# Where the first loads of a two-layer LoRA kernel are held: the second half of block 0 and the experts' weights

## The chip, the cores and the metric

The kernel runs on one NeuronCore of one Trainium2 chip. The metric is the device time of one execution in microseconds (us), lower is better. Of the kernel before there are three timed runs, and one further execution was recorded by the hardware profiler.

## The reference

`x` holds 64 sequences of 64 tokens with 1024 features, in float32. Layer 0 adds to every sequence the output of its own rank-16 adapter; layer 1 adds a dense layer and a mixture of eight rank-16 experts, of which the two with the largest logits are used for each token.

```python
# layer 0: A, B chosen for each sequence by itok_B_4_50
Bx = einsum('bni,bri->bnr', x, B[ids0]);  x = x + einsum('bnr,bor->bno', Bx, A[ids0])
# layer 1: language_ids = itok_B_0_7
base   = einsum('btd,od->bto', x, W)
logits = einsum('btd,ed->bte', x, Wr) + 5.0 * one_hot(language_ids)
gates  = two largest logits of each token, softmax over the two
h      = einsum('btd,erd->bter', x, A)
x = x + base + 2.0 * einsum('bter,bte,eor->bto', h, gates, B)
```

## The kernel before

The 4096 tokens are cut into eight blocks of 512. Tokens are columns: a block of `x` is 1024 features by 512 tokens, held as two tiles `("x", k, 0)` and `("x", k, 1)` of four feature groups each (1 MB a tile). Two feature groups are a quarter of a block, 512 KB. The blocks are worked in four pairs. For each pair the dense layer is a fast matrix product with seven block products instead of eight (the tiles `ti`, `t`, `s`, `sf`, `pa`, `pb`, `pf` belong to it); for the first pair one product is done whole (`pw`).

For each block, in the order of the data:

- `gather` on POOL brings 128 rows of `B` (`gb`) and of `A` (`ga`), 512 KB each, by indirect DMA.
- `turn`: TensorE transposes `gb` (`pt`), ScalarE copies it out (`bt`).
- `project`: TensorE multiplies `bt` with the first and then the second half of the block (`pb`), VectorE masks the result (`bx`).
- `adapt`: TensorE multiplies `ga` with `bx` (`px`), VectorE adds it into `x`.
- `rows`: TensorE multiplies the adapted `x` with the experts' weights `a1_sb` (`ph`), ScalarE copies `h`; then `gates` on VectorE, and `weigh` transposes on TensorE (`pg`).

The order in which each engine issues its work is not written by hand. Every step is given to `Plan.add` with its engine and cost, the keys that it reads and writes, a due number `at` (lower is more urgent), buffers that it takes, and, for a DMA, its size. `Plan.order` (lines 64 to 167) plays these through once: at each turn it takes the engine that can start first and, among its steps that can start within `LOOK` = 0.2 of that, the one with the lowest `at`. A DMA's end is set by one running total (`moved`, 350 KB a unit of time) plus `LAND` = 1.8. The result is a fixed program order on each engine; what the chip then does with it, it does in its own time, and an instruction whose input is late holds up all behind it on its engine.

At the start the order of the loads is steered with small copies on POOL that wait for one DMA and write one column into the target of the next, so that the next DMA's issue on SP must wait for the copy:

- `hold` in `load` (line 368) keeps the whole second half of block 0 until the first quarter of block 0 has landed.
- `hold` in `consts` (line 316) keeps the experts' weights `a1_sb` until `gb` of block 0 has landed. The first pieces of `W`, `x` of block 1 and the gathers of block 1 are all put behind the issue of that load (`behind=[("a1",)]`, lines 322, 394, 420, 653).

SP's queue issues in program order: ids, the two quarters of the first half, `wr_c`, `ids1`, the second half, `a1_sb`, two pieces of `W`, both halves of block 1, then the other 14 pieces of `W` (256 KB each) and `b1_sb`. Three VectorE steps (`add_identity`, line 655) add the identity into the diagonal pieces of `W` when they are there: w11, w22 and w33 follow w00.

Of the kernel before, what the change touches and what calls it, by code (L numbers as in the profile page):

```python
# [14 lines left out]
P = 128  # L15
# [159 lines left out]
def kernel(  # L175
# [52 lines left out]
    TB = 512  # L228
# [5 lines left out]
    HC = NC // 2  # L234
# [19 lines left out]
    act, pool, sp = Pinned(tc, nc.scalar), Pinned(tc, nc.gpsimd), Pinned(tc, nc.sync)  # L254
# [6 lines left out]
    plan = Plan(slots, {"l"})  # L261
# [7 lines left out]
    def new(tag, shape, name):  # L269
        return pools[tag].tile(shape, F32, tag=tag, name=name)  # L270
# [16 lines left out]
    half = const.tile([P, 1], F32, name="half")  # L287
# [7 lines left out]
    a1_sb = const.tile([P, NC, P + E], F32, name="a1_sb")  # L295
# [13 lines left out]
    def consts():  # L309
        plan.add({"SP": 0.4}, lambda e: sp.dma_start(wr_c, wr), [], [("wr_c",)], -53, kb=8)  # L310
        plan.add(
            {"SP": 0.4}, lambda e: sp.dma_start(ids1_sb, ids1[0:1, :].to_broadcast([P, NB])),
            [], [("ids1",)], -53, kb=32,
        )

        def hold(e):

            pool.tensor_copy(a1_sb[:, 0, :1], made["gb", 0][:, :1])

        plan.add({"POOL": 0.2}, hold, [(("gb", 0),)], [("a1",)], -56)  # L320
        plan.add({"SP": 0.4}, lambda e: sp.dma_start(a1_sb[:, :, :P], a1), [], [("a1",)], -45, kb=512)
        plan.add({"SP": 0.4}, lambda e: sp.dma_start(b1_sb, b1), [], [("b1",)], -29, kb=512, behind=[("a1",)])

        def spread(e):
            pool.tensor_copy(a1_sb[:, :, P:], wr_c)

        plan.add({"POOL": 0.3}, spread, [("wr_c",)], [("wr",)], -45)
# [24 lines left out]
    made = {}  # L352

    def part(t, cs=range(HC), gs=range(NG)):
        return [(t, c, g) for c in cs for g in gs]
# [7 lines left out]
    def load(k, i, at):  # L363
        t = ("x", k, i)

        held = (k, i) == (0, 1)

        def hold(e):

            made[t] = new("q", [P, HC, TB], f"x_{k}_{i}")  # L370
            pool.tensor_copy(made[t][:, 0, :1], made["x", 0, 0][:, 0, :1])


        cuts = ((0, HC // 2), (HC // 2, HC)) if (k, i) == (0, 0) else ((0, HC),)

        def fn(c0, c1):
            if not held and c0 == 0:
                made[t] = new("q", [P, HC, TB], f"x_{k}_{i}")
            sp.dma_start(
                made[t][:, c0:c1],  # L380
                xT[(i * HC + c0) * P : (i * HC + c1) * P, k * TB : (k + 1) * TB].rearrange(
                    "(c p) t -> p c t", p=P
                ),
            )

        if held:
            plan.add(
                {"POOL": 0.2}, hold, part(("x", 0, 0), [0]), part(t), at, [("q", t)]
            )
        for c0, c1 in cuts:  # L390
            plan.add(
                {"SP": 0.5}, lambda e, c0=c0, c1=c1: fn(c0, c1),
                [], part(t, range(c0, c1)), at, [("q", t)] * (not held and c0 == 0),
                kb=256 * (c1 - c0), behind=[("a1",)] * (k == 1) + [(t, 0, 0)] * (c0 > 0),
            )
# [359 lines left out]
    def fine_weights(s, n, k, a, at):  # L755
# [33 lines left out]
        if s == FINE:  # L789
            for x in range(4):  # L790
                plan.add(
                    {"DVE": 0.29, "POOL": 0.48}, sums(x), [(a,)] + [(t, y) for y in range(x)], [(t, x)], at - 3,
                    [("s", t)] * (x == 0), sb=True,
                )
            plan.add({"SP": 0.1}, keep, [(t, x) for x in range(4)], [("fine", n, k)], at + 4, kb=256)
        else:
            plan.add({"SP": 0.1}, load, [("fine", n, k)], [(t, x) for x in range(4)], at - 6, [("s", t)], kb=256)
# [462 lines left out]
    for k, at in ((0, -60), (1, -42)):  # L1260
        load(k, 0, at)
        gather(k, "gb", b0, at - 1)
        load(k, 1, at)
        gather(k, "ga", a0, at)
        if k == 0:
            consts()
# [81 lines left out]
```

## Time and profile before

| | us |
|---|---|
| median of three runs (lowest, highest) | 515.6 (515.04, 516.07) |
| the profiled execution, its own time | 514.86 |
| its span, first to last instruction | 513.0 |
| TensorE busy in the span | 499.8 |
| first matmul begins at | 8.80 |

The span is the time from the first to the last instruction; the rest of the execution's own time, 1.86 us, lies around it. All times below are counted from the start of the span. In the rows, L29 is a helper that every instruction goes through, so the work is told apart by the names of tiles: `x<-in_xT` is a load of x, `gb<-in_b,idx` the gather of B, `a_sb<-in_a` the load of the experts' weights. POOL rows named COPY with one column are the holds.

### The profile page before, as it was taken

The page shows a single profiled execution, that of the slowest core. Times are in us where ns is not written, and L with a number is a line of the kernel's source. Part 1 is how long each engine was busy: PE and PEld are TensorE (multiplying, and loading weights), DVE is VectorE, ACT ScalarE, POOL GpSimd, SP SyncE. Part 2 cuts the span into 40 slices and gives each one's busy share as a digit, 9 for nine tenths or more (in the row PEclk, how much of TensorE's full clock was granted, in tenths as well). Part 3 has the DMA queues.
Part 4 walks back from the last instruction along what each step waited for, and adds up shares of the span by engine and source line. Part 5 has one row for each costly group of instructions (what it writes and reads, how often), then busy time and mean ns, then how long its engine had stood idle before and what let it go on. Part 6 is the DMA issues. An engine that isn't in the chain of part 4 may idle for free.

```text
span 513.0 us, 9559 instructions
## 1 busy us (share of the span) xinstructions
PE 499.8 (97%) x3678; PEld 442.5 (86%) x3678; DVE 410.3 (80%) x822; ACT 75.8 (15%) x204; POOL 105.4 (21%) x175
## 2 busy tenths in 40 slices
PE   3999999999999999999999999999999999999997
PEld 2857888889888998889888998889989999999996
DVE  0788899989878777888989789874889988875964
ACT  1111100001000211111201221102301112112210
POOL 3002000020432433442233021201212120212100
PEclk9999999999999999999999999999999999999999
DMA  8999273964895648875567645972756665673023
GB/s 286 374 369 351 83 270 120 332 247 141 300 312 201 208 130 284 309 247 187 185 226 236 221 131 173 356 260 81 240 173 205 231 202 142 228 192 96 0 115 132
DMA packets 60172, 110.00 MB, mean 214 GB/s; under 512 B 5600, under 2 KB 11744, under 8 KB 60128
## 3 DMA queue, kind: packets, MB, share of 16 engines
q1 hardware_dynamic: 57824, 101.01, 58.7%
q0 software_dynamic: 2304, 8.39, 4.9%
q8 instruction: 29, 0.48, 0.4%
q14 instruction: 15, 0.12, 0.1%
HBM read 76.09 MB, written 33.29 MB: 213 GB/s over the span
## 4 chain that ended last, share of the span: by engine, by line
PE 94%; DMA 4%; DVE 1%; issue 0%; SPq 0%
PE pa L29 38%; PE pb L29 19%; PE pf L29 16%; PE ph L29 12%; PE px L29 3%; PE pw L29 3%; DMA x<-in_xT 3%; PE pt L29 2%; DMA gb<-in_b,idx 1%; PE pg L29 1%; DVE s L29 0%; DMA ids_sb<-in_ids 0%; DVE ti L29 0%; DVE u L29 0%; DVE x L29 0%
## 5 line engine op out<-in xcount | busy, mean ns | idle before, releaser
L29 PE MATMUL pa<-ti,s 128*128 128x256 f32 x432 | 102.1, 380 | 0.0
L29 PEld LDWEIGHTS pa<-ti,s 128*128 128x128 f32 x432 | 78.7, 190 | 9.3
L29 ACT COPY cp<-pf 128x128 f32<-128x128 f32 (+1 forms) x123 | 37.0, 302 | 214.4 <-PE pf L29 201.3
L29 PEld LDWEIGHTS ph<-a_sb,x 128*128 128x128 f32 x512 | 61.7, 190 | 1.5 <-issue 0.9
L29 PE MATMUL ph<-a_sb,x 128*128 128x136 f32 x512 | 62.5, 279 | 0.2 <-issue 0.2
L29 PE MATMUL pb<-ti,s 128*128 128x256 f32 x224 | 55.8, 380 | 0.0
L29 PE MATMUL pa<-x,s 128*128 128x256 f32 x216 | 52.7, 381 | 0.0
L29 PE MATMUL pf<-tt,sf 128*128 128x128 f32 x246 | 47.5, 277 | 0.0
L29 DVE TENSOR_TENSOR x<-px,x 128x512 f32<-128x512 f32 x64 | 39.9, 683 | 6.8 <-PE px L29 6.8
L29 PEld LDWEIGHTS pb<-ti,s 128*128 128x128 f32 x224 | 40.9, 190 | 4.8 <-issue 0.2
L29 PEld LDWEIGHTS pf<-tt,sf 128*128 128x128 f32 x246 | 41.4, 191 | 3.8 <-issue 0.4
L29 PEld LDWEIGHTS pa<-x,s 128*128 128x128 f32 x216 | 39.3, 190 | 5.0 <-issue 0.4
L29 PE MATMUL pa<-t,s 128*128 128x256 f32 x168 | 41.2, 380 | 0.0
L29 PEld LDWEIGHTS pa<-t,s 128*128 128x128 f32 x168 | 30.8, 190 | 3.9 <-issue 0.2
L29 POOL TENSOR_TENSOR tt<-ti 128x256 f32<-128x256 f32 x16 | 12.3, 771 | 93.5 <-PE pf L29 60.2
L29 DVE TENSOR_TENSOR o<-pa,u 128x512 f32<-128x512 f32 x32 | 22.0, 687 | 9.9 <-PE pa L29 9.6
L29 POOL TENSOR_TENSOR tt<-x 128x256 f32<-128x256 f32 x11 | 9.2, 833 | 93.9 <-PE pf L29 47.7
L29 DVE TENSOR_TENSOR o<-pb,o 128x512 f32<-128x512 f32 x35 | 23.1, 687 | 2.7 <-PE pb L29 1.9
L29 DVE TENSOR_TENSOR ti<-t 128x512 f32<-128x512 f32 x24 | 16.7, 696 | 8.4 <-PE pb L29 6.4
L29 DVE TENSOR_TENSOR ti<-x,ti 128x512 f32<-128x512 f32 x30 | 21.7, 724 | 1.2 <-PE pb L29 0.6
L29 DVE TENSOR_TENSOR o<-o,cp 128x256 f32<-128x256 f32 x46 | 19.6, 425 | 2.5
L29 POOL TENSOR_TENSOR sf<-s 128x128 f32<-128x128 f32 x27 | 14.0, 518 | 35.8 <-DMA s<-s_kept 14.5
(154 smaller groups left out, 807.6 us busy)
## 6 DMA issues: line engine op xcount, KB each, us to landing
s<-s_kept SPq DMA_DIRECT2D x147, 256.0 KB
x<-in_xT SPq DMA_DIRECT2D x15, 1024.0 KB
out_T<-o SPq DMA_DIRECT2D x30, 512.0 KB
s_kept<-s SPq DMA_DIRECT2D x28, 256.0 KB
sf<-f_kept SPq DMA_DIRECT2D x27, 256.0 KB
s_kept<-w SPq DMA_DIRECT2D x18, 256.0 KB
w<-in_w SPq DMA_DIRECT2D x16, 256.0 KB
f_kept<-sf SPq DMA_DIRECT2D x14, 256.0 KB
```

Of the source, the lines that this page charges most:

```text
L29: return self._tc.keep_in_program_order(f(*args, **kwargs))
```

## The change

In block 0 all four quarters are loads of their own: the second half, until now one DMA of 1 MB, becomes two of 512 KB. The hold in front of them now waits for the landing of block 0's second quarter instead of its first. The hold in front of the experts' weights now waits for the landing of the third quarter instead of `gb` of block 0. Nothing else is edited; the planner orders all steps anew.

```diff
         def hold(e):
-            pool.tensor_copy(a1_sb[:, 0, :1], made["gb", 0][:, :1])
+            pool.tensor_copy(a1_sb[:, 0, :1], made["x", 0, 1][:, 0, :1])
-        plan.add({"POOL": 0.2}, hold, [(("gb", 0),)], [("a1",)], -56)
+        plan.add({"POOL": 0.2}, hold, part(("x", 0, 1), [0]), [("a1",)], -56)
...
-        def hold(e):
-            made[t] = new("q", [P, HC, TB], f"x_{k}_{i}")
-            pool.tensor_copy(made[t][:, 0, :1], made["x", 0, 0][:, 0, :1])
-        cuts = ((0, HC // 2), (HC // 2, HC)) if (k, i) == (0, 0) else ((0, HC),)
+        half = HC // 2
+        def hold(c0, by):
+            def fn(e):
+                if c0 == 0:
+                    made[t] = new("q", [P, HC, TB], f"x_{k}_{i}")
+                pool.tensor_copy(made[t][:, c0, :1], made["x", 0, 0][:, by, :1])
+            return fn
+        cuts = ((0, half), (half, HC)) if k == 0 else ((0, HC),)
...
-                {"POOL": 0.2}, hold, part(("x", 0, 0), [0]), part(t), at, [("q", t)]
+                {"POOL": 0.2}, hold(0, half), part(("x", 0, 0), [half]), part(t), at, [("q", t)]
```

## The prediction

> **What bounds the kernel now.** I read the page first, then the waits of TensorE, then the timeline of the first 45 us, then the DMA queues in narrow windows.
>
> ```profile
> span 513.0 us, 9559 instructions
> PE 499.8 (97%) x3678; PEld 442.5 (86%) x3678; DVE 410.3 (80%) x822; ACT 75.8 (15%) x204; POOL 105.4 (21%) x175
> ```
>
> TensorE is busy for 499.8 of 513.0 us. Of the 13.2 us in which it is not, one wait makes most (waits of PE, whole span; total, times, longest; the next in that list is 0.4):
>
> ```profile
> PE pt L29 <- DMA gb<-in_b,idx: 8.8, 1, 8.8
> ```
>
> So a change of the first loads can help only by starting the first transpose (pt) earlier, and can hurt by opening a gap behind it. The timeline (start, us, engine, operation, idle before and its releaser) has all the steps concerned:
>
> ```profile
> 3.08 1.11 POOL L29 DMA_INDIRECT gb<-in_b,idx  x1 [1.31 <-DVE order L29]
> 5.06 0.18 POOL L29 COPY x<-x 128x1 f32<-128x1 f32 x1 [0.87 <-DMA x<-in_xT]
> 5.27 0.38 SPq L29 DMA_DIRECT2D x<-in_xT  x1
> 5.40 0.97 POOL L29 DMA_INDIRECT ga<-in_a,idx  x1 [0.16 <-issue]
> 6.59 0.24 POOL L29 COPY a_sb<-wr_c 128x64 f32<-128x64 f32 x1 [0.22 <-issue]
> 8.71 0.18 POOL L29 COPY a_sb<-gb 128x1 f32<-128x1 f32 x1 [1.88 <-DMA gb<-in_b,idx]
> 8.80 1.94 PE L29 MATMUL pt<-ident,gb 128*128 128x128 f32 x8 [8.80 <-DMA gb<-in_b,idx]
> 8.93 0.66 SPq L29 DMA_DIRECT2D a_sb<-in_a  x1
> 9.04 0.97 POOL L29 DMA_INDIRECT gb<-in_b,idx  x1
> 10.67 3.40 PE L29 MATMUL pb<-x,bt 128*32 128x128 f32 x64
> 14.50 2.07 PE L29 MATMUL px<-bx,ga 32*128 32x128 f32 x64 [0.42 <-DVE bx L29]
> 16.49 1.25 PE L29 MATMUL pt<-ident,gb 128*128 128x128 f32 x8
> 17.93 7.65 PE L29 MATMUL ph<-a_sb,x 128*128 128x136 f32 x64 [0.19 <-issue]
> ```
>
> The chain is gb landed (8.66), pt, pb, px, the second block's pt, ph, and from 18 us on TensorE has no gap: in the windows 18 to 60 us it is busy 42.00 of 42. The DMA engines meanwhile are full from 2 us to beyond 40 (share about 1.0, 350 to 400 GB/s in most windows).
>
> **The change, part by part.**
>
> *Second half held longer.* The hold waits for the second quarter. In the semaphore records the first quarter is complete at 5.00; the second has 14 of its 16 increments recorded, the last at 6.09, so I take 6.2 (6.1 to 6.5). With the present offset from landing to issue (5.00 to 5.27) SP issues the third quarter near 6.5 and the fourth, 0.45 later (a half-megabyte issue takes 0.41 to 0.46), near 6.9, against 5.27 for both. Does gb then land earlier? Two windows of the queue rows, 7 to 8 us and 8 to 9.5 us (q1 is SP's queue, q0 POOL's; packets, MB, share):
>
> ```profile
> q1 hardware_dynamic: 113, 0.23, 64.0%
> q0 software_dynamic: 51, 0.15, 36.6%
> ...
> q1 hardware_dynamic: 286, 0.59, 101.9%
> q0 software_dynamic: 3, 0.01, 1.4%
> ```
>
> The Trainium skill, "DMA: Bandwidth & Descriptors", section "Queues, rings and completion order", says that an engine takes turns between the queues that have work, packet by packet. By that rule x takes half of every engine from gb after 7 us; without it the 0.15 MB that gb still has would pass in 0.4 us at 373 GB/s, gb would be through at 7.4 instead of 8.2 and TensorE would start some 0.7 us earlier. The rows speak against it: ga's gather was issued by 6.37, yet from 8 to 9.5 us POOL's queue moves almost nothing while x moves 0.59 MB; ga follows only after x. Work is served in the order of arrival. gb arrived before x, and its last packets come 0.155 us apart, their own length (159 ns), so x isn't between them. I take 0 for gb, with -0.7 as the lower end; above, a gather that landed 0.1 later would cost 0.1.
>
> *What the hold leaves idle.* x's first packets move at 7.09, as the first engines finish gb. SP's first x load needed 1.06 us from issue (1.19) to its first packet (2.25); issued at 6.5 the third quarter moves from about 7.5. The fast engines idle 0.2 to 0.4 us; the engine that finishes gb last (about 8.2) none. A landing is that of the slowest engine, so the fourth quarter should be complete where the half is now (11.77), at most 0.4 later. pb reaches the second half in the middle of its 3.40 us, at 12.4, and its last quarter at 13.2: slack of 1.0 to 1.4 us. Cost 0 (up to 0.2).
>
> *POOL's order.* With the hold at 6.2 the planner lets the copy of wr_c go before ga's gather: wr_c is estimated at 6.65, the hold ends at 6.83, ga must wait for the third quarter's issue (7.13). So ga is issued near 7.0 instead of 5.40. It stays behind x in the engines' order, as now, and lands near 12.7 to 13.1 (now 12.7); px wants it at 14.5. Cost 0.
>
> *Experts' weights behind the third quarter.* The third quarter needs 16 packets of 84 ns per engine, 1.35 us, after gb on the slow engine (8.2), and some 0.5 to land: 10.0 to 10.4. Copy and issue as now (0.27): a1 at 10.3 to 10.6 instead of 8.93, gb of block 1 at 10.4 to 10.8 instead of 9.04, everything on SP behind them issued 1.4 to 1.7 later. The cover is the backlog: third and fourth quarter and ga keep a fast engine busy until 7.5 + 2.7 + 1.3 = 11.5, and a1's packets come at 10.3 + 1.06 = 11.4. So the stream of loads shifts by 0 to 0.4 us, not by 1.4. First user is the second pt at 16.49: its gb lands at 15.64 now (issue 9.04 plus 6.6), slack 0.85. If nothing covers, it lands at 17.0 to 17.4 and TensorE loses 0.5 to 0.9. I take 0.1, as gb's place in the order is the same as now. a1 also lands at 15.64, and ph starts at 17.93.
>
> *VectorE's order.* In the planner the second half ends later (13.7 instead of 10.9), so all compute of the first blocks moves by 2.8 of its units, the loads only by 1.3. Seen from compute, W comes 1.5 earlier, and the urgent identity adds (at -30) move ahead: w11 before the last ti, w22 and w33 each ahead of one more of the adds into x of block 1. On the chip W does not come earlier:
>
> ```profile
> 23.93 0.69 DVE L29 TENSOR_TENSOR ti<-x,ti 128x512 f32<-128x512 f32 x1
> 26.04 0.19 DVE L29 TENSOR_TENSOR l<-h,bias 128x32 f32<-128x32 f32 x1 [1.43 <-ACT h L29]
> 27.67 0.28 DVE L29 TENSOR_TENSOR bx<-pb,mask 128x128 f32<-128x128 f32 x1
> ```
>
> w11 completes at 26.43 in the semaphore records, w22 at 33.13, w33 at 35.34. VectorE will stand from about 24 to 26.7, then do w11 (0.48), ti (0.65) and the gates: bx moves from 27.67 to about 29.0, the gated h from 30.42 to 31.8, the w22 stop adds little. What covers this: px of block 1 uses bx only at 31.03 (2 us), pg uses h at 35.67, and the adds into x of block 1 begin at 41.0 instead of 40.83 against ph at 44.28. Cost 0. Without that cover it would be the 1.3 us of the stop.
>
> Later steps keep their order: planner clocks that matter there all move by the same amount. Equal times that round differently could still swap a few steps.
>
> Sum: 0 + 0 + 0 + 0.1 + 0 = +0.1 us on a profiled execution of 514.86 (span 513.0 and 1.86 around it). That execution is 0.74 under the median, so I carry the difference to the median: 515.6 + 0.1 = 515.7.
>
> **The rivals.** 0.2% is 1.03 us, about what a measurement of this kernel can tell from no change (its three runs lie 1.03 apart).
>
> *A, gb gains from an undisturbed queue* (taking turns): -0.4 to -0.7, 514.9 to 515.2. Against it stands the silence of ga behind x. To pass 0.2% it would need more than the 0.8 that gb could save; only a shorter cold phase on top could do it.
>
> *B, the second pt waits for its gb,* which follows its issue one for one: +0.5 to +0.9, 516.1 to 516.5. For it: POOL's gather is issued 1.4 later. Against: the full engines.
>
> *C, slower: TensorE pauses while its clock is low.* pb of block 0 runs at half speed (64 matmuls with a median of 421 ns; those of block 1 take 272 to 280, and 1.96 us in all instead of 3.40); the clock record turns to full at 13.7 us, 4.9 after the first matmul. "TensorE: Matmul & The Clock Gate", section "Part 1: The HAM clock gate", says that the array runs at half clock until one window of about 3.4 us was busy. If the fourth quarter lands after 13.2, pb waits for it inside that window; the window may not count as busy, and up to another 3.4 us of work run at half speed: 1.7 us, plus a wait of 0.3 or more. That gives 517.3 to 518. It decides itself at a landing of 13.2 and a wait of some tenths. Taking turns between ga and the fourth quarter would bring it there: 0.5 MB more ahead of it are 1.3 us, 13.1 instead of 11.8.
>
> *D, swapped steps later in the plan* open or close gaps of a microsecond in a TensorE that has 4.4 us of gaps in all: -1 to +2.
>
> **How the numbers follow.** No visible effect (my sum, -0.4 to +0.6): 0.58. A: 0.10. B: 0.14. C: 0.10. D: 0.08. Of these, faster by over 0.2%: half of D's better side, an A with a lucky clock window, and spread of the runs, 0.08. Slower: C, half of D, the upper end of B with spread of the runs, 0.20. Within: 0.72. The range from 514.5 to 517.2 holds A, my sum and B with half a microsecond for the spread of the runs, and leaves out most of C and the ends of D.
>
> **What would show it.** Right: first pt at 8.8, ±0.2; third quarter issued near 6.5; a_sb's issue at 10.3 to 10.6; second pt within 0.3 of 16.5; ph near 18; VectorE idle from 24 to 26.7 with an add into w next; no PE wait over 0.5 us but the first. Wrong: pt before 8.2 (A); an idle before the second pt released by gb (B); pb longer than 4 us, or px after 15.5 (C); gaps behind 60 us that are not there now (D).

## The result, and the profile after

The changed kernel is slower. Its median over five runs is 520.51 us (518.61 to 521.02), that of the kernel before, run beside it, 515.76 (515.04 to 516.07): a ratio of 1.0086 with a 95% interval of 1.0074 to 1.0098. The forecast was 515.7 with a range up to 517.2. The profiled execution took 518.61, the shortest of the five, with a span of 516.5 against 513.0 before. So of 4.7 us in the medians the profile can show only 3.5; the other executions of the five were 1.3 to 2.4 us longer still.

TensorE's waits in the changed kernel (total, times, longest):

```profile
PE pt L29 <- DMA gb<-in_b,idx: 10.0, 2, 8.7
PE pa L29 <- DVE o L29: 1.2, 1, 1.2
PE pa L29 <- DVE w L29: 0.9, 1, 0.9
```

The first wait is still 8.7 us long, but it now occurs twice: the second block's pt waits for its gather too. The two others did not exist before. The timeline of the start (start, us, engine, operation, idle before and its releaser), the same rows as were shown of before:

```profile
6.52 0.18 POOL L29 COPY x<-x 128x1 f32<-128x1 f32 x1 [2.48 <-DMA x<-in_xT]
...
6.72 1.06 SPq L29 DMA_DIRECT2D x<-in_xT  x2
7.08 0.97 POOL L29 DMA_INDIRECT ga<-in_a,idx  x1
8.70 1.94 PE L29 MATMUL pt<-ident,gb 128*128 128x128 f32 x8 [8.70 <-DMA gb<-in_b,idx]
...
10.57 3.24 PE L29 MATMUL pb<-x,bt 128*32 128x128 f32 x64
...
11.18 0.18 POOL L29 COPY a_sb<-x 128x1 f32<-128x1 f32 x1 [3.13 <-DMA x<-in_xT]
11.39 0.66 SPq L29 DMA_DIRECT2D a_sb<-in_a  x1
11.86 0.97 POOL L29 DMA_INDIRECT gb<-in_b,idx  x1 [0.50 <-issue]
...
17.59 1.06 PE L29 MATMUL pt<-ident,gb 128*128 128x128 f32 x8 [1.29 <-DMA gb<-in_b,idx]
```

Up to pb the start is as before. Then the hold of a_sb ends at 11.18 instead of 8.71, gb of block 1 is issued at 11.86 instead of 9.04, and the second pt begins at 17.59 instead of 16.49: 1.1 us lost. What the DMA engines did meanwhile stands in the windows (window, its length, busy time of PE, PEld, DVE, ACT, POOL, then the granted clock, DMA share, GB/s; the record of the clock begins only at 13.26 us, so the 1.00 before that is no reading). The changed kernel:

```profile
7.50:8.50 1.00, 0.00 (x0) 0.00 (x0) 0.00 (x0) 0.00 (x0) 0.55 (x1) 1.00 0.65 158
8.50:9.50 1.00, 0.80 (x4) 0.83 (x5) 0.00 (x0) 0.00 (x0) 0.00 (x0) 1.00 0.85 287
...
12.50:14.50 2.00, 1.58 (x42) 1.26 (x36) 0.29 (x1) 0.00 (x0) 0.33 (x1) 1.00 0.68 200
```

The same three in the kernel before:

```profile
7.50:8.50 1.00, 0.00 (x0) 0.00 (x0) 0.00 (x0) 0.00 (x0) 0.00 (x0) 1.00 1.02 377
8.50:9.50 1.00, 0.70 (x4) 0.73 (x5) 0.00 (x0) 0.00 (x0) 0.64 (x2) 1.00 1.04 403
12.50:14.50 2.00, 1.58 (x37) 1.21 (x29) 0.29 (x1) 0.00 (x0) 0.00 (x0) 1.00 1.05 370
```

So there are two holes: one behind each of the two longer holds.

The remaining 2.5 us are lost further on. First VectorE stops, in program order, at an add into W that has not landed. Later VectorE wants the buffer of a store of `o` that has not landed, and TensorE waits for VectorE:

```profile
28.38 0.49 DVE L29 TENSOR_TENSOR w<-w,ident 128x128 f32<-128x128 f32 x2 [4.63 <-DMA w<-in_w]
...
139.24 0.39 SPq L29 DMA_DIRECT2D out_T<-o  x1
...
147.24 0.69 DVE L29 TENSOR_TENSOR o<-pa,v 128x512 f32<-128x512 f32 x1 [5.23 <-DMA out_T<-o]
...
156.71 1.99 PE L29 MATMUL pa<-ti,s 128*128 128x256 f32 x8 [1.20 <-DVE o L29]
```

The store is itself no later than in the kernel before (issued at 139.24 and landed at 147.15, against 139.61 and 147.88): VectorE asks for its buffer sooner in the new order.

Laying the matmuls of both traces side by side, TensorE of the changed kernel is 1.1 us behind from 17.6 us on, 1.8 to 2.2 behind from 74 us on (after the wait for w), and 3.6 behind from 175 us to the end (after the wait for o).

### The profile page after: what moved, and what is told of

Read it like the earlier page. It is cut to its first block, busy times and chain, and to the rows that moved or that the text cites. A ratio compares the mean times of both kernels' runs of the same rounds, so it can differ in the third digit from the quotient of the medians.

```text
span 516.5 us, 9562 instructions
## 1 busy us (share of the span) xinstructions
PE 500.3 (97%) x3678; PEld 442.1 (86%) x3678; DVE 409.5 (79%) x822; ACT 76.2 (15%) x204; POOL 104.5 (20%) x175
## 4 chain that ended last, share of the span: by engine, by line
PE 82%; DMA 8%; DVE 6%; SPq 3%; issue 1%; POOL 0%; DVEq 0%; POOLq 0%
PE pa L29 37%; PE pb L29 17%; PE pf L29 16%; PE ph L29 8%; DMA w<-in_w 3%; DMA x<-in_xT 3%; PE px L29 3%; SPq L29 3%; DMA out_T<-o 2%; DVE t L29 1%; PE pt L29 1%; DVE ti L29 1%; DVE o L29 1%; DVE x L29 1%; DVE m L29 1%
## 5 line engine op out<-in xcount | busy, mean ns | idle before, releaser
L29 DVE TENSOR_TENSOR ti<-x 128x512 f32<-128x512 f32 x30 | 21.9, 731 | 0.1
```

The source lines that it names most:

```text
L29: return self._tc.keep_in_program_order(f(*args, **kwargs))
```

## The experiments

Each kernel was run in the same job as the kernel before, and its ratio is to that. "Order of before" or "of after" means the program order that the planner gave to that kernel; it can be kept while the data that a hold really waits for is changed. "Later" for ga means that four small copies on POOL go ahead of it (issued 1.41 us after x in e11, against 0.14 in e8). The ratio is worked out over all executions, not from the medians: in e8, whose executions fall into two groups, the medians are 5.0 us apart and the means 3.4. Code is shown in substance, with arguments written out. The medians:

| kernel | order | x held by quarter | a_sb held by | ga | median (lowest to highest) | ratio, 95% interval |
|---|---|---|---|---|---|---|
| e7 split only | before | 1, two loads | gb | as before | 515.76 (514.83 to 516.51) | 0.9989 [0.9979, 0.9999] |
| e14 the same again | before | 1, two loads | gb | as before | 515.55 (514.43 to 516.60) | 0.9987 [0.9978, 0.9996] |
| e2 order only | after | 1, one load | gb | as after | 516.64 (514.72 to 518.33) | 1.0013 [1.0002, 1.0025] |
| e3 x held | before | 2, two loads | gb | as before | 518.21 (515.28 to 520.17) | 1.0037 [1.0022, 1.0053] |
| e4 a_sb held | before | 1, two loads | quarter 3 | as before | 516.37 (515.83 to 518.86) | 1.0009 [0.9996, 1.0021] |
| e1 both held | before | 2, two loads | quarter 3 | as before | 518.57 (517.63 to 519.53) | 1.0050 [1.0032, 1.0068] |
| e8 x held, one load | before | 2, one load | gb | as before | 521.11 (514.62 to 522.43) | 1.0059 [1.0035, 1.0083] |
| e11 e8, ga late | before | 2, one load | gb | later | 516.69 (515.24 to 519.22) | 1.0012 [1.0001, 1.0022] |
| e16 e8, ga first | before | 2, one load | gb | ahead of the hold | 516.37 (514.81 to 518.51) | 1.0005 [0.9994, 1.0016] |
| e15 split, ga late | before | 1, two loads | gb | later | 515.78 (514.78 to 517.87) | 0.9992 [0.9979, 1.0005] |
| e13 e1, ga late | before | 2, two loads | quarter 3 | later | 518.76 (516.17 to 520.96) | 1.0049 [1.0031, 1.0066] |
| e9 changed kernel again | after | 2, two loads | quarter 3 | as after | 519.26 (517.19 to 520.95) | 1.0059 [1.0038, 1.0080] |
| e12 it, ga late | after | 2, two loads | quarter 3 | later | 518.39 (518.03 to 520.54) | 1.0045 [1.0029, 1.0060] |
| e10 it, a_sb as before | after | 2, two loads | gb | as after | 518.02 (514.52 to 521.94) | 1.0036 [1.0017, 1.0055] |
| e17 it, ga first | after | 2, two loads | quarter 3 | ahead of the hold | 518.72 (517.39 to 521.61) | 1.0067 [1.0041, 1.0092] |
| e18 e10, ga first | after | 2, two loads | gb | ahead of the hold | 516.00 (514.50 to 517.86) | 0.9994 [0.9983, 1.0005] |

### The parts, one by one

e7 and e14 keep both holds of before and only cut the 1 MB load in two:

```diff
-            lambda e: fn(c0, c1)
+            lambda e: [fn(0, half), fn(half, HC)]       # the second half of block 0
```

> Old program order and old holds (first quarter, gb); only the second half of block 0 is loaded by two DMAs of 512 KB instead of one of 1 MB. 'Idle DMA' theory (the loss of e3_x_hold_only comes from DMA engines that ran empty at 7.5 to 8.5 us and start again slowly): 0, within 0.3 us. 'Split' theory (ga of block 0 gets between the two halves on some engines, so the fourth quarter lands at 13 to 14 and pb waits): most of e3's +1.9 us is here, +1 to +2.

> The two half loads alone, with the holds and the program order of before, once more (first time: ratio 0.9989, interval 0.9979 to 0.9999). If splitting the load is worth something, the ratio is below 1 again, 0.998 to 0.9995; if that was spread, 0.9995 to 1.001.

The split costs nothing; twice the ratio lies just below 1, by 0.11 and 0.13%. No other version's interval lies below 1, and the gain is less than what a single measurement could tell.

e2 has the program order of after with the holds and the single load of before:

```diff
# in the changed kernel; the planner still sees the new holds; the joining of the two loads is left out here
-                pool.tensor_copy(made[t][:, c0, :1], made["x", 0, 0][:, half, :1])
+                pool.tensor_copy(made[t][:, c0, :1], made["x", 0, 0][:, 0, :1])
-            pool.tensor_copy(a1_sb[:, 0, :1], made["x", 0, 1][:, 0, :1])
+            pool.tensor_copy(a1_sb[:, 0, :1], made["gb", 0][:, :1])
```

> The changed kernel's program order on every engine, but the old waits (first quarter, gb) and one load of 1 MB. Theory 'late loads': 0, at most +0.5 us over the kernel before. Theory 'new order': +2.4 us, the part of the profile's 3.5 that appears after 59 us, up to +3.7.

0.6 us, barely apart from nothing. e3, e4 and e1 are the other way round: order of before, with one hold changed, the other, or both.

```diff
# e3 and e1: x of block 0, second half, behind the second quarter
+                pool.tensor_copy(made[t][:, c0, :1], made["x", 0, 0][:, half, :1])
# e4 and e1: a_sb behind the third quarter
+            pool.tensor_copy(a1_sb[:, 0, :1], made["x", 0, 1][:, 0, :1])
```

> Old program order; only the second half of block 0 is changed: two loads behind the second quarter's landing; the experts' weights stay behind gb. Both theories: within 0.3 us of the kernel before. If the half load itself is what lands too late, +0.5 or more.

> Old program order; only the experts' weights are changed: behind the third quarter's landing, which is loaded behind the first quarter as before. The third quarter should land near 10, a1 be issued near 10.3 and gb of block 1 near 10.4. Late loads: between the kernel before and e1_holds_only, +0.3 to +1.5 us. New order: 0 to +0.5.

> All of the change's waits and its two half loads, but every engine keeps the program order of the kernel before (the planner is shown the old dependencies). Theory 'late loads' (gb of block 1, a1 and W follow the third quarter one for one, and TensorE waits for them): nearly the whole loss is here, +3.5 to +5 us over the kernel before. Theory 'new order' (the planner, shown later ends, mixes steps differently up to 190 us, and that costs): here only the wait of the second pt remains, +1.1 us (16.49 to 17.59 in the changed kernel), at most +1.5.

The holds make most of the loss, not the order: e1 is 2.5 us slower, e3 2.2, and e4 0.3, which its interval does not tell from nothing. In e3's profile the fourth quarter is complete only at 14.57 us in the semaphore records, and pb and px read in the timeline:

```profile
14.61 0.64 PE L29 MATMUL pb<-x,bt 128*32 128x128 f32 x16 [1.49 <-DMA x<-in_xT]
...
15.67 3.28 PE L29 MATMUL px<-bx,ga 32*128 32x128 f32 x64 [0.41 <-DVE bx L29]
```

The last quarter of pb waits 1.5 us, and px then takes 3.28 us where before it took 2.07: the clock had been full from 12.89 us in the clock record, and the window shows what it was afterwards (third number from the right):

```profile
16.50:19.50 3.00, 3.00 (x51) 2.77 (x46) 1.84 (x3) 0.00 (x0) 0.19 (x1) 0.50 1.06 382
```

So the pause costs about twice: the wait, and a stretch of 3.41 us at half speed behind it. That is rival C in another form: C let the clock rise later, here it had risen and fell back. In e1, e8 and e9 it does rise later, as C has it: the record turns to full at 20.00, 21.02 and 18.15 us instead of 13.70.

### Is it the clock?

e5 and e6 put 30 transposes of the identity ahead of everything on TensorE, so that its clock is full when the first gather lands; e5 is the kernel before, e6 the changed one.

```diff
+    for i in range(30):
+        pe.transpose(warm[:, i % HC, :], ident, ident)
     plan.issue()
```

> The kernel before with 30 extra 128x128 transposes of the identity on TensorE while it waits for the first gather (they fill a PSUM tile that nobody reads). 'Clock' theory (the first 5 us of TensorE's work run at half clock, and what ends that phase depends on how busy TensorE was in a free-running window): pt and pb of block 0 take about 1.0 and 2.0 us instead of 1.94 and 3.40, so -1.5 to -2.4 us against the kernel before, and less scatter from run to run. If the first loads alone set the pace: 0.

> The changed kernel with the same 30 transposes. 'Clock' theory with late loads: pb gets faster but waits for the fourth quarter, pt of block 1 still waits for its gb (landed 17.5), so only the scatter from lost clock windows goes: 517 to 519 us, some 1.5 to 3 below the changed kernel, still 2 to 4 above e5. If the loss is all clock: equal to e5 within 0.5. If the clock plays no part: 520.

e5 took 516.03 (ratio 1.000, 0.999 to 1.001), so the 1.5 to 2.4 us that were expected of it did not come; in its profile the clock falls back to half from 10.87 to 17.70 us, so pb and px ran at half speed after all. e6 took 519.38 (1.0061, 1.0042 to 1.0079). In e6 the clock is full from 5.3 to 15.5 us and the loss stays: pb waits 3.1 us for x, the second pt 1.8 for gb. There a faster TensorE only waits longer for the same loads. The low clock enlarges the pause; the late loads make it.

### Why x is late

e8 has nothing but the longer hold of x, still as one load of 1 MB:

```diff
-            pool.tensor_copy(made[t][:, 0, :1], made["x", 0, 0][:, 0, :1])
+            pool.tensor_copy(made[t][:, 0, :1], made["x", 0, 0][:, half, :1])
```

> Old program order, one DMA of 1 MB for the second half, a1 behind gb; only the hold of the second half waits for the second quarter instead of the first. 'Idle DMA': +1 to +2 us, as e3_x_hold_only. 'Split': within 0.5 us of the kernel before. The DMA rate from 7.5 to 8.5 us should be 160 to 200 GB/s in either case.

Its executions fall apart into two groups: 5 of 22 took 514.6 to 516.0, the others 517.3 to 522.4. The profiled execution is one of 521.50:

```profile
6.14 0.38 SPq L29 DMA_DIRECT2D x<-in_xT  x1
6.28 0.97 POOL L29 DMA_INDIRECT ga<-in_a,idx  x1 [0.16 <-issue]
...
16.96 1.94 PE L29 MATMUL pb<-x,bt 128*32 128x128 f32 x32 [4.58 <-DMA x<-in_xT]
```

Its window of the DMA engines has the same hole as the changed kernel:

```profile
7.50:8.50 1.00, 0.00 (x0) 0.00 (x0) 0.00 (x0) 0.00 (x0) 0.01 (x1) 1.00 0.62 170
```

The sixteen semaphore increments of the x load come in two groups (one for each engine that finishes its share, as the Trainium skill has it in "DMA: Bandwidth & Descriptors", section "Why a DMA increments its semaphore by 16 and not by 1"): twelve by 11.48 us, the last four at 13.94, 15.17, 16.72 and 16.82. Those of ga, issued 0.14 us after x, are all there by 13.75. So on four engines ga, though issued later, was through before x. There are two readings: ga arrived at these engines ahead of x, or a queue that had run dry is taken up late whatever else there is. e11 delays ga by four small copies on POOL, e16 issues it ahead of the hold:

```diff
# e11
+            for _ in range(4):
+                pool.tensor_copy(wait, ident)
             pool.indirect_dma_start(out=made["ga", 0], ...)
# e16, in the hold of x; the later gather of ga is then left out of its place
+                bring()                                  # the gather of ga, block 0
                 pool.tensor_copy(made[t][:, c0, :1], made["x", 0, 0][:, half, :1])
```

> Program order of before, one load of 1 MB, held by the second quarter (the kernel that took 521.1 in the median and whose x was complete on four of sixteen engines only at 13.9 to 16.8), and POOL does four small copies ahead of the gather ga, so that it is issued about 1 us later. Theory 'overtaken by ga': x is then ahead of ga on every engine, complete at 11.5 to 12.5, nearly every execution at 515 to 517. Theory 'slow restart': the engines take up x late because SP's queue had run dry, whatever ga does; x is complete at 13 or later on some engine and the median stays at 519 or more.

> The same single load held by the second quarter, but POOL issues ga ahead of the hold's copy, near 4.1 instead of 6.3, so that ga is ahead of x on every engine. Theory 'order of arrival': x is complete at 12.5 to 13.5 on all engines (ga's half megabyte is 1.3 us), pb waits about 1 us for it: 516.3 to 518, and no executions at 521. Theory 'a restarted queue loses against the other': x is again complete at 14 to 17 on some engine, median 519 or more.

> The control: two half loads with the holds and the order of before, and the four copies ahead of ga, so that the fourth quarter is ahead of ga (in the split kernel ga was issued between the two). If ga's delay costs or gains nothing by itself, 515.5 to 516.5, as the split kernel, and the gain of 4 us that it brought under the long hold is due to x being overtaken there. If a late ga by itself gives time back, 514.5 to 515.3; if px waits for it, 516.5 to 517.5.

Both take nearly the whole loss away: from 521.1 to 516.7 and 516.4 (in the ratios from 1.0059 to 1.0012 and 1.0005). And ga's delay gives nothing by itself (e15, the control, is as the split kernel). In e16 ga fills the engines while x is held, and x is complete on all sixteen between 11.78 and 13.19:

```profile
4.48 0.94 POOL L29 DMA_INDIRECT ga<-in_a,idx  x1 [0.30 <-issue]
...
6.34 0.38 SPq L29 DMA_DIRECT2D x<-in_xT  x1
...
13.32 1.08 PE L29 MATMUL pb<-x,bt 128*32 128x128 f32 x32 [0.56 <-DMA x<-in_xT]
```

```profile
7.50:8.50 1.00, 0.00 (x0) 0.00 (x0) 0.00 (x0) 0.00 (x0) 0.00 (x0) 1.00 1.01 414
```

That is the forecast of "order of arrival": behind all of ga, x is late by little and on every engine alike. In e11 x is still later on four engines (12.94 to 13.43) than on the other twelve (by 11.85), so a part of the scatter is there without ga ahead. And in e8 the last engines are 3.6 us behind the latest of e16; ga alone, half a megabyte, is 1.3 us.

The packets in e8's trace show that neither reading is the whole. x moves on 7 of the 16 engines at 8.25 us, on 13 at 8.75 and on all 16 only at 9.75, so some engines took it up two microseconds late. By then ga is there too, and on these engines the two do not go one behind the other but alternate, packet by packet. (On a busy engine a packet is recorded as beginning 3 or 4 ns before the end of the one before it, so it can be counted what follows what; chance hits are subtracted, and the counts are good to about 5.) Of the 87 packets of x that begin after 12 us, about 35 are followed by another of x and about 35 by one of a gather. Four engines that alternate packets of 84 and 159 ns give x 4 x 84/243 = 1.4 engines' time; the trace has x on 1.0 to 1.5 engines from 11.25 to 12.75 us. gb of block 1 (issued at 8.81) shares in it: POOL's queue moves all of it, 0.52 MB, while x is not yet complete (window 13.5 to 16.5; packets, MB, share):

```profile
q1 hardware_dynamic: 740, 0.61, 62.2%
q0 software_dynamic: 144, 0.52, 44.7%
```

Alternating alone costs nothing. In e7 and e14, which lose nothing, about 118 and 116 of x's 512 packets are followed by one of ga; in e3 it is 89, in e8 48, in the kernel before 26, in e9 16. In e11 and e16 and in the first profile of the changed kernel it is 5 or fewer. What costs is that some engines take x up late and then have to share their time. What decides whether the queues alternate was not found.

### The changed kernel itself

e9 runs it again. e12 delays ga in it, e13 in e1, with the edit of e11. e10 gives a_sb its old hold, e17 puts ga first, e18 does both.

> The changed kernel itself, once more, beside its variants. Its profiled execution so far was its fastest (518.61), the median 520.5; what the slower ones do is not seen. Theory 'overtaken': in them the gather ga is served ahead of the third or fourth quarter on one or more DMA engines, x is complete only at 13 to 15 us, and TensorE's pb waits 1 us or more for it; so a profile of a median execution shows that wait. Theory 'later part': the start is alike in all (second pt waits 1.1 us for its gb, nothing else), and the difference lies behind 60 us, in waits for w and for a store. Median 519.5 to 521 by both.

> The changed kernel with the same four copies ahead of ga, which is then issued about 1 us later still. Theory 'overtaken': the slower executions go, median 518 to 519 (what is left is the second pt's wait for gb and the later waits). Theory 'slow restart' or 'later part': 520 to 521 as the changed kernel. If ga itself comes too late for px (needed at 14.2), a wait of px for ga shows, up to 1 us.

> Both longer holds and the two half loads in the program order of before (the kernel that took 518.6, +2.5), with ga issued about 1 us later. If the +2.5 is x overtaken by ga at the start, most of it goes: 516.4 to 517.2, pb's wait for x under 1 us. If the late issue of a_sb, gb and W carries as much by itself, 518 or more, with the second pt waiting for its gb.

> The changed kernel with its own program order, its two half loads and its longer hold of x, but the experts' weights held by gb of block 0 again, as before the change. If the loss is the sum of two separate things, the hold of x (start) and the late issue of a_sb, gb and W (second pt, later the waits for w and o), this gives back the second: issue of a_sb at 8.7 to 8.9, second pt at 16.5, median 517 to 518. If the late x alone makes the loss, it stays at 519.5 to 521.

> The changed kernel with ga issued ahead of the hold's copy, so that the engines have work while x is held and x follows ga in order. Theory 'two terms' (x loses engines to ga; a_sb, gb and W follow the third quarter): the first term is gone, the second is not: the third quarter lands at 11 to 11.5, gb of block 1 at 17.5 to 18.5, the second pt waits 1 to 2 us, 517.3 to 518.8. If the hold of x alone makes the loss, 516 to 516.9. If the program order has a large part, it stays at 519 or more.

> The same with a_sb held by gb of block 0 again: of the change only the longer hold, the split and the program order are left. By 'two terms' both are gone and only the order's 0.6 is left: 516.3 to 517, no execution above 519 (without ga ahead, the same kernel went from 514.5 to 521.9). If the long hold costs by itself, whatever is ahead of x, 517.5 or more.

e9's profiled execution (518.48) lost its time elsewhere than the first one: thirteen engines have the fourth quarter by 12.91, the next two at 13.52 and 14.26, one increment is missing from the records; TensorE is 3.5 us behind at the second pt and the same 3.5 behind at the end:

```profile
14.30 1.08 PE L29 MATMUL pb<-x,bt 128*32 128x128 f32 x16 [0.86 <-DMA x<-in_xT]
15.80 3.16 PE L29 MATMUL px<-bx,ga 32*128 32x128 f32 x64 [0.41 <-DVE bx L29]
20.03 1.06 PE L29 MATMUL pt<-ident,gb 128*128 128x128 f32 x8 [1.07 <-DMA gb<-in_b,idx]
```

It is three things: pb waits 0.9 us for x, px takes 3.16 us instead of 2.07 because the clock record turns to full only at 18.15 us, and the second pt waits 1.1 us for its gb. So this execution has rivals C and B at once. "Overtaken" and "later part" were both partly right: the place of the loss changes from one execution to the next.

e18 and e17 divide it. With ga first and a_sb held by gb, nothing is left of the loss (0.9994), although the longer hold of x, the split and all of the new program order are still in it. With ga first and a_sb behind the third quarter, 2.6 us are left in the medians (ratio 1.0067). In e17 x is in order, the third quarter is complete at 12.56, and behind it there is nothing left for the engines to do:

```profile
12.69 0.18 POOL L29 COPY a_sb<-x 128x1 f32<-128x1 f32 x1 [5.89 <-DMA x<-in_xT]
...
13.37 0.96 POOL L29 DMA_INDIRECT gb<-in_b,idx  x1 [0.50 <-issue]
...
19.33 0.84 PE L29 MATMUL pt<-ident,gb 128*128 128x128 f32 x6 [1.35 <-DMA gb<-in_b,idx]
```

```profile
12.50:14.50 2.00, 2.00 (x44) 1.87 (x40) 0.00 (x0) 0.14 (x1) 1.15 (x2) 1.00 0.11 36
```

The DMA engines stand for most of two microseconds (36 GB/s), and the second pt waits for its gather. This is rival B.

So there are two ways to a loss of about 2 us: the hold of x by way of pb (e10: 1.7 in the median, 514.5 to 521.9), and the hold of a_sb by way of the second pt (e17: 2.6). The second needs a late third quarter: with x held as before the hold of a_sb costs 0.3 (e4, third quarter complete at 10.91 us against 12.56 in e17). Both together are not their sum (e1: 2.5; e9: 2.9), and an explanation is that where pb is late, the second pt needs its gather later too. It would also explain why delaying ga helped e8 by 4.4 us in the median, but e13 not at all (518.76 against 518.57): in e13's profile the second pt waits 1.8 us instead, and starts 0.13 us after its gb has landed.

The later waits come with the order of after. e12 and e13 start alike (second pt 1.6 and 1.8 us late), but at the end e13, in the order of before, is 1.9 us behind and e12 4.3. In e18's profile, an execution of 517.75, TensorE again waits 1.2 us for o at the same place although a_sb was not held by the third quarter; most executions of e18 (18 of 22) took 516.6 or less. So the new order can lose this microsecond or two and often does not. What decides it was not found.

## Why the prediction was wrong, point by point

- *Second half held longer*: right in its times. The second quarter landed at 6.46 (6.2 forecast, up to 6.5), the third was issued at 6.72. That gb gains nothing is right for the two profiles that were compared (first pt at 8.70 against 8.80), but not for the others: in the ten profiles with the longer hold of x and ga not first, gb lands at 8.42 to 8.83 us; in the seven with the old hold at 8.66 to 9.92, with a median of 9.44, and the one that the prediction was read from is the earliest of these. So a gain like rival A's, about 0.9 us between the medians, is there, and the late loads take back more. How a load issued behind gb delays it is not shown: x does not alternate with gb in the kernel before.
- *What the hold leaves idle*: this is the first step that failed, put at 0 (up to 0.2). It had fast engines idle for 0.2 to 0.4 us and took the landing as at most 0.4 later. Measured over the two windows from 7.5 to 9.5, the engines moved 158 and 287 GB/s instead of 377 and 403: 0.34 MB less, 0.9 us of a full rate. The fourth quarter was complete at 12.54 in the first profile (0.77 later than the half before), and at 14.26 or later in e9. The step took SP's one time from issue to first packet (1.06 us) for all sixteen engines; with a share of 0.65 and then 0.85 they take the load up one after another over two microseconds (x moves on 8 engines at 8.0 us, 11 at 8.5, 14 at 9.0, all 16 at 9.75).
- *POOL's order*: the issue at 7.08 was as forecast (near 7.0), px waited for ga in neither profile of the changed kernel, and in the first of them ga did stay behind x. But "work is served in the order of arrival" was taken for a rule from one stretch of one trace, and it is not one: e16 fits it, in e7, e14 and e8 x and ga alternate. The silence of POOL's queue from 8 to 9.5 us could not decide between the two. With alternation and engines that start late, the fourth quarter lands late (14.57 in e3), as the prediction's own last sentence on rival C has it.
- *Experts' weights behind the third quarter*: the second step that failed, and the larger of the two in the first profile. The third quarter landed at 11.05 (10.0 to 10.4 forecast), gb of block 1 was issued at 11.86 and not at 10.4 to 10.8, and the backlog that should have covered it was gone (200 GB/s from 12.5 to 14.5). The term was put at 0.1, with 0.5 to 0.9 if uncovered; it was 1.1 in the first profile, 1.6 in e17 (2.84 behind at the second pt, 1.27 at the first). The two steps were costed as if independent, while the first one's delay is the second one's start.
- *VectorE's order*: the stop came where it was forecast, at w11, but took 4.6 us instead of 2.7, since W is issued behind a_sb (w11 complete at 28.35, 26.43 before). bx was written at 31.21 instead of 29.0. The cover then ended in a wait for w of 0.9 at about 63 us. "Later steps keep their order" was wrong: of the 822 places in VectorE's order, 298 hold an instruction with other names than before, the last of them the 480th. That by itself costs 0 to 0.6 us (e18, e2), but with late loads it lost 2.5 in the profile (rival D's place), more than the second pt did.
- *The rivals*: B and C both happen, in changing shares, and C was priced nearly right at 517.3 to 518 (e3: 518.2, e1: 518.6); its mechanism, a clock that rises a window later, is in e1, e8 and e9. They were given 0.14 and 0.10 as if each needed its own accident. They share a cause, the hold that lets the engines run dry (e16 and e18, where ga fills them, lose nothing), and should have been one case with the larger share.

What stays open: no profile shows an execution of the changed kernel at its first median of 520.5; the longest one seen in profile is 518.61. What happens in the others is inferred from e8, e9 and e12. Nor is it known why some engines take a load up two microseconds later than others.

## What to carry to other kernels

A hold that waits for the landing of the last load in its own queue leaves that queue without work for the whole way from landing to the first packet of the next load (6.46 to 7.74 us here), and the engines too once the other queue's transfer is through; wait for the load before it, or give the engines other work that is needed anyway (here ga ahead of the hold took the loss away). Before a landing is costed as "the same engines, a little later", ask which transfer of another queue will share the engines with it. And where a second hold hangs on the first one's data, cost the two as one chain, with the backlog recomputed after the first delay.

## What the hardware showed that was not expected

- TensorE's clock falls back. In e3 the record turns to full at 12.89 us, to half at 16.30, and to full again at 19.71: steps of 3.41 us. In e5 the warmed clock is full from 7.46 to 10.87 and half from 10.87 to 17.70, although TensorE was busy for 5.28 of the 6.5 us from 11.0 to 17.5. The Trainium skill, "TensorE: Matmul & The Clock Gate", section "Part 1: The HAM clock gate", has windows of about 3.4 us, which agrees. But the page lets the clock fall after an idle window; here it fell after stretches in which TensorE was busy for 1.50 of 3.41 us (e3, 12.89 to 16.30) and 1.60 (e5, 7.46 to 10.87), with no pause longer than 1.5 us in e3. Cutting the first 26 us of all 20 profiles into stretches of 3.41 us that end at the changes of the record gives both limits. The clock fell after the four stretches with 1.60 us of work or less and stayed full after the 53 with 1.65 or more; it rose after 24 stretches with 2.74 us or more and stayed at half after 41 with 2.75 or less (matmul ends are modelled, so the 0.01 of overlap means nothing). That is why pb's pause of 0.9 us in e9 cost a whole stretch at half speed: it left 2.55 us of work in its stretch.
- The sixteen engines are not served alike. One load of 1 MB was complete on its first engine at 10.55 us and on its last at 16.82 (e8), and with the same issue but other neighbours between 11.78 and 13.19 (e16).
- Two queues can alternate on one engine packet by packet (e7, e8, e14), and the same two queues can go strictly one behind the other (e11, e16).
- The landing of the first gather moves by more than a microsecond: 8.42 us in e3's profile, 8.66 before, 9.33 and 9.92 in the two profiles of the split kernel. A part of this goes with what is issued behind it (8.42 to 8.83 under the longer hold, 9.21 to 10.03 where ga goes first); between the two of the split kernel it is scatter. In the later of these TensorE is 1.0 us behind at the end (515.88, against 514.83 in the other), so a part of the spread of these kernels is there at the first matmul.
